# Gated attention and mixture block: batch 1's keys first, a third base summed early, copies and loads moved to other queues

## The chip, the cores and the metric

The kernel runs on one core of a Trainium2 chip. The metric is the device time of one execution in microseconds, the median over several runs. Five engines work side by side, each through its own instructions in order: TensorE (PE in the profile; PEld is its weight load), VectorE (DVE), ScalarE (ACT), GpSimd (POOL) and SyncE (SP). DMAs are issued by instructions that stand in the queue of SP, ScalarE or GpSimd.

## The reference

Eight batches of 256 tokens, 512 wide, all float32. Each goes through a gated attention and a gated mixture of experts:

```python
x = x + tanh(g_xattn) * attention(layernorm(x), context)
x = x + tanh(g_ffn) * mixture(layernorm(x))
```

The attention has 32 query heads and 8 key and value heads of 16. Queries come from the context and x together; keys and values once from x and once from the context. A query sees the 64 latest positions of both, with a bias that falls with distance, through one softmax. The mixture has 8 bases (gate, up and SiLU, 256 wide) that are mixed for each token by weights from a router (128 experts, the best 4), then a common down projection, and a shared expert of 512 that is handled as two more pieces of 256.

## The kernel before, in words

**Order of the work.** The program is written as generators: `attention(b)`, `project(b)`, `tail(b, t)`, `feed_forward(b)`, `first_weights()` and a few more. Each yields planned durations; `start` scales them to a stretch of planned time, and `run` always advances the generator that is due first. This planned time only decides the order in which instructions are written to the engines' queues. On the chip each engine takes its queue in order and waits at an instruction until its inputs and buffers are ready.

**Stages.** For a batch: `project` normalises x, transposes it, and forms keys (`pk`), queries (`pq`, four groups) and values (`pv`). Each result lies in a PSUM bank (`ps_one`, tag "one") until ScalarE has copied it out. `put_values` writes the values to `vpad`, and `diagonals` copies them by DMA (16 copies of 128 KB per batch) into `vbd`, a block-diagonal layout. `attention` takes 8 groups of scores (`sc`) in 16 steps: VectorE adds the bias and takes the maximum (L641), ScalarE does the exponential (L660), VectorE the reciprocal (L669), GpSimd the division (L672), VectorE the transpose (L685), TensorE the product with `vbd` (L707). `tail` projects the output (`po`, L866), normalises again, transposes (`tr_f`), and computes the router (`pl`, `pst`, `pc`). Then `feed_forward` computes 10 pieces (8 bases, 2 shared) with seven block products instead of eight, by sums of tokens (`sT`) and sums of weights.

**The first batches.** `project_first` does part of batch 0 directly. What is left of batch 0's projections, and then all of batch 1's, is a generator `rest` that `first_batch` (batch 0's attention) advances with `piece`, one part between two softmax steps at a time. Batch 0's attention thus runs beside the projections of batches 0 and 1, and the first feed-forward beside batch 1's attention and batch 2's projections.

**Sums of weights.** A piece of gate and up weights is four blocks of 256 KB (groups 1 to 4), and four sums of them are needed. `sub` forms a sum, `keep` stores it to DRAM; later batches load what is stored (`load_gu`). In `first_weights` bases 2, 0 and 1 are loaded and summed on GpSimd during the first softmax (`first_sums`). The pieces from 3 on are summed in the first feed-forward: `more` and `late` in `feed_forward` place `sub(k + 1, ...)`, two on VectorE and two on GpSimd, and the stores. Weight buffers are double; `after` loads piece i + 2 into a buffer as soon as TensorE has read piece i.

**The queues.** SP issues nearly all loads and stores from about 25 us on, in order: weights, stores of sums, the 16 copies to `vbd` of batches 1 to 7 and half of batch 0's (the other half is GpSimd's), and inputs of batches 2 to 7. ScalarE's queue issues the first weights and batch 1's inputs at the start. The line numbers in the profile before are those of this listing.

Of the kernel before, what the change touches and what calls it, by code (L numbers as in the profile page):

```python
# [37 lines left out]
def gated_block(  # L38
# [229 lines left out]

    def first_weights():

        for k in (2, 0, 1):
            for g in range(1, 5):
                load_gu(k, g)
            if k == 2:
                yield 2.0
                later["wd"] = weight(w_down, I, HID, "wd", nc.sync)


                later["sd"] = sd = const.tile([P, NSI // 2, HID], F32, tag="sd", name="sd")
                nc.sync.dma_start(  # L280
                    sd, sw_down.rearrange("(j o p) n -> o p j n", o=2, p=P)[1]
                )
            if k == 0:
                yield 5.5
                yield from first_sums(2)
        yield 1.0
        yield from first_sums(0)
        yield 1.0
        yield from first_sums(1)

    def first_sums(k):
        sub(k, 1, nc.gpsimd)
        yield 1.0
        sub(k, 3, nc.gpsimd)
        keep(k, 1)
        yield 1.0
        sub(k, 2)
        keep(k, 3)
        yield 1.0
        sub(k, 4)  # L300
        keep(k, 2)
        yield 1.0
        keep(k, 4)
        summed.add(k)
# [69 lines left out]
    def project_first():  # L374
# [62 lines left out]
        def rest():  # L437
            banks = [0]

            def own(name):  # L440
                banks[0] += 1
                if banks[0] % 2:
                    return other_bank(2, name)
                return ps_one.tile([P, 2 * T], F32, tag="one", name=name)

            pv = own("pv_0").rearrange("p (t s n) -> p t s n", t=NT, s=2)
            for t in range(NT):
                yield BEFORE if t == 0 else MORE
# [24 lines left out]
            ready.add("queries")  # L473
            yield from project(1, xns)
# [13 lines left out]
            yield fill[1]  # L488
            fill[1] = next(fill[0], None)

    def diagonals(qd, eng):


        for g in range(G):
            at = D * (1 - g % 2)
            eng.dma_start(
                vbd[g * Q : (g + 1) * Q, qd].rearrange("p a k r -> p a (k r)"),
                vpad[qd * Q : (qd + 1) * Q, :, at : at + 2 * HK * D],
            )
# [7 lines left out]
    def project(b, xns=None):  # L507
        def own():
            yield from hold(0.0 if b == 1 else GAP)
# [5 lines left out]
        if b > 1:  # L515
            while b > 2 and b - 3 not in stored:
                yield 0.5
            loaded[b] = load(b), load_context(b)
            yield 16.0
        xt, ctT = loaded[b]  # L520
        if xns is None:
# [2 lines left out]
            xns = normed()  # L524
            yield 3.0
        xnT = two.tile([P, NC, T], F32, tag="xo", name=f"xnT_{b}")
        if b == 1:
            yield BEFORE
        for t in range(NT):
            yield from own()  # L530
            evict = transposed(xnT, xns[t], t, f"x{b}", bank)
            yield AFTER if b == 1 else AFTER - 0.8
            evict()
            free()
            yield BEFORE if b == 1 else BEFORE + 0.8


        kT = two.tile([P, 2, 2, T], F32, tag="kT", name=f"kT_{b}")
        yield from own()
        pk = bank([P, 2, T], f"pk_{b}")  # L540
        for s, (w_sb, src) in enumerate(((wsk_sb, ctT), (wk_sb, xnT))):
            for c in range(NC):
                nc.tensor.matmul(  # L543
                    pk[:, s, :], lhsT=w_sb[:, c, :], rhs=src[:, c, :],
                    start=(c == 0), stop=(c == NC - 1),
                )
            yield AFTER if s else MORE
        for par in range(2):
            for s in range(2):
                nc.scalar.activation(  # L550
# [1 line left out]
                )  # L552
        free()
        yield BEFORE


        qT = two.tile([P, NB, G, Q], F32, tag="qT", name=f"qT_{b}")
# [34 lines left out]
    def attention(b):  # L592
# [185 lines left out]
        for u in range(2 * n + 4):  # L778
            i, j = divmod(u, 2)
            m = i // 2 - 1 if i >= 3 and i % 2 else None  # L780
            if j == 0:
                if i < n:
                    scs = score(i)
                elif m is not None:
                    scs = [bank(f"sc_{b}_{i}_{p}") for p in range(2)]
            if m is not None:
                values(m, j, pts[m], scs)
            exponentials()
            if i < n:
                nmax = memory(u)  # L790
            yield 1.0

            for step, ps in enumerate(((2,), (3,), (0, 1))):
                if u in (1, 2) and step < 2:
                    diagonals(2 * (u - 1) + step, nc.sync)
                exponentials()
                for p in ps:
                    if i < n:
                        soften(i, j, p, scs, prs[u], nmax, dens[u])
                if step == 0 and 0 <= u - 1 < 2 * n:  # L800
                    divide((u - 1) // 2, (u - 1) % 2, prs[u - 1], dens.pop(u - 1))
# [170 lines left out]
    def feed_forward(b):  # L972
# [120 lines left out]


        for k in range(PIECES):
            late = b == 0 and k > 2
            more = b == 0 and 2 < k + 1 < PIECES
            if k == NK:
                shT = one.tile([P, NSI, T], F32, tag="shT", name=f"shT_{b}")
            one_and_five(k)  # L1100
# [137 lines left out]
    project_first()  # L1238
    start(attention(0), 0.38, at=-0.585, total=70.0)
    start(after_diagonals(), 0.2, at=-0.535, total=1.0)  # L1240
    start(first_weights(), 0.39, at=-0.537, total=20.5)
    start(attention(1), 0.86, at=FIRST, total=74.1)
    at = -0.2
    while 0 not in sides:
# [52 lines left out]
```

## Time and profile before

| | |
|---|---|
| median of 3 runs | 1021.93 us (1018.09 to 1021.96) |
| profiled execution, its own time | 1023.29 us |
| its span | 1021.4 us |
| mean granted TensorE clock | 0.992 |
| busy: TensorE, VectorE, ScalarE, GpSimd | 989.7, 601.0, 442.0, 470.2 us |
| DMA, mean over the span | 188 GB/s |

The profile is one execution. A group's row gives line, engine, operation, output and input names, then busy time or start and length, and in brackets the wait just before it with the engine that ended it. SPq, ACTq and POOLq are the issues of DMAs; the rows of a queue's waits give the waiting line, what it waited for, the total, how often, and the longest. The time from issue to landing of a DMA is in the list of DMA issues. A clock below 1.00 in a window means that TensorE ran slower there.

### The profile page before, as it was taken

How to read it: one execution, taken by the hardware profiler on the slowest of the kernel's cores; microseconds unless marked ns; L12 is line 12 of the kernel's file. 1: busy time of each engine (PE TensorE's matmuls, PEld its weight loads, DVE VectorE, ACT ScalarE, POOL GpSimd, SP SyncE). 2: the span in 40 equal slices, each digit the busy share in tenths (PEclk: the TensorE clock that was granted, in tenths of full speed). 3: DMA queues.
4: the chain of work that ended last, by engine and by line, in shares of the span. 5: the costliest groups of instructions: out<-in, count | busy, mean ns of one | idle time of the engine just before them, and what ended most of it. 6: DMA issues, size and time to landing. Idle time of an engine off the chain costs nothing.

```text
span 1021.4 us, 27843 instructions
## 1 busy us (share of the span) xinstructions
PE 989.7 (97%) x10470; PEld 799.9 (78%) x10470; DVE 601.0 (59%) x2241; ACT 442.0 (43%) x1657; POOL 470.2 (46%) x892
## 2 busy tenths in 40 slices
PE   8888799899999999999999999999999999999998
PEld 8666687777888687886778868788787977787886
DVE  2764766757564675636855378544665466765453
ACT  3652454335542455415543255433554335442231
POOL 4773576734553255523644236342455225661341
PEclk9999999999999999999999999999999999999999
DMA  6942845569545694447844577455964468665891
GB/s 206 231 145 79 252 146 151 170 199 288 175 137 154 180 301 142 152 141 217 282 141 146 163 214 256 125 166 165 267 204 140 133 191 257 203 195 174 271 302 66
DMA packets 117302, 192.15 MB, mean 188 GB/s; under 512 B 12848, under 2 KB 34864, under 8 KB 117168
## 3 DMA queue, kind: packets, MB, share of 16 engines
q1 hardware_dynamic: 112672, 184.87, 58.9%
q10 hardware_dynamic: 4112, 4.46, 1.3%
q8 instruction: 83, 1.36, 0.5%
q0 software_dynamic: 384, 1.05, 0.5%
q14 instruction: 51, 0.42, 0.1%
HBM read 158.87 MB, written 14.68 MB: 170 GB/s over the span
## 4 chain that ended last, share of the span: by engine, by line
PE 87%; DVE 5%; issue 2%; POOL 2%; ACT 2%; DMA 1%; SPq 0%; ACTq 0%; DVEq 0%; POOLq 0%
PE m L1001 38%; PE m L1010 10%; PE pq L562 8%; PE sc L707 6%; PE po L866 5%; PE sc L628 5%; PE pd L1144 4%; PE pk L543 2%; PE pv L582 2%; PE pd L1147 2%; POOL pr L672 1%; PE pq L402 1%; PE pl L896 1%; DVE pr L641 1%; ACT pr L660 1%
## 5 line engine op out<-in xcount | busy, mean ns | idle before, releaser
L672 POOL TENSOR_SCALAR pr<-pr,rd 128x192 f32<-128x192 f32 (+2 forms) x512 | 210.9, 430 | 251.6 <-DVE rd L669 234.3
L660 ACT ACTIVATE pr<-pr,nm 128x192 f32<-128x192 f32 (+2 forms) x512 | 218.9, 430 | 110.0 <-DVE nm L641 58.7
L1001 PE MATMUL m<-w,sT 128*128 128x256 f32 x1024 | 253.1, 381 | 1.1 <-DMA w<-in_L_ffn_w_up 0.7
L1001 PEld LDWEIGHTS m<-w,sT 128*128 128x128 f32 x1024 | 194.5, 191 | 29.0 <-issue 1.2
L641 DVE CUSTOM_DVE_ANT_1 pr<-sc,nbias 128x192 f32<-128x192 f32 (+2 forms) x512 | 154.0, 322 | 99.8 <-PE sc L628 92.9
L1001 PE MATMUL m<-w,hT 128*128 128x256 f32 x768 | 204.9, 390 | 1.0 <-DVE u L1046 1.0
L1001 PEld LDWEIGHTS m<-w,hT 128*128 128x128 f32 x768 | 140.1, 191 | 25.6 <-issue 6.3
L1091 POOL TENSOR_TENSOR mixed<-mixed,th 128x256 f32<-128x256 f32 x112 | 81.2, 725 | 137.8 <-DVE th L1086 137.8
L685 DVE STREAM_TRANSPOSE pt<-pr 128x768 f32<-128x768 f32 (+2 forms) x128 | 111.5, 871 | 4.6 <-POOL pr L672 3.0
L660 ACT ACTIVATION_READ_ACCUMULATOR pr<-pr,nm 128x1 f32 x512 | 97.9, 191 | 0.0
L1047 POOL TENSOR_TENSOR m<-m,u 128x256 f32<-128x256 f32 x80 | 61.2, 765 | 67.8 <-DVE u L1046 58.9
L963 ACT ACTIVATE th<-m 128x256 f32<-128x256 f32 x80 | 30.8, 384 | 138.2 <-DVE up L1057 138.1
L707 PEld LDWEIGHTS sc<-pt,vbd 64*32 64x32 f32 x5120 | 61.1, 106 | 26.3 <-issue 14.2
L707 PE MATMUL sc<-pt,vbd 64*32 64x64 f32 (+2 forms) x5120 | 69.0, 229 | 9.1 <-DVE nm L641 5.2
L1069 DVE TENSOR_TENSOR gate<-u,m 128x256 f32<-128x256 f32 x80 | 33.3, 416 | 72.4 <-PE m L1001 66.9
L1057 DVE TENSOR_TENSOR up<-u,m 128x256 f32<-128x256 f32 x80 | 33.3, 417 | 67.6 <-PE m L1001 40.7
L628 PE MATMUL sc<-kT,qT 32*128 32x192 f32 (+2 forms) x1024 | 64.9, 336 | 4.6 <-DVE nm L641 4.1
L628 PEld LDWEIGHTS sc<-kT,qT 32*128 32x128 f32 x1024 | 45.1, 184 | 28.3 <-DVE nm L641 9.4
L963 ACT ACTIVATE th<-gate 128x256 f32<-128x256 f32 x80 | 33.2, 416 | 76.7 <-DVE gate L1069 76.7
L1010 PE MATMUL m<-sT,w 128*128 128x128 f32 x512 | 66.1, 278 | 0.0
L1010 PEld LDWEIGHTS m<-sT,w 128*128 128x128 f32 x512 | 62.3, 194 | 0.4
L1144 PE MATMUL pd<-sd,shT 128*128 128x512 f32 x128 | 61.5, 603 | 0.2 <-DVE shT L1080 0.2
(131 smaller groups left out, 1375.7 us busy)
## 6 DMA issues: line engine op xcount, KB each, us to landing
w<-s SPq DMA_DIRECT2D x284, 256.0 KB, 3.5
w<-in_L_ffn_w_gate SPq DMA_DIRECT2D x130, 256.0 KB, 3.1
w<-in_L_ffn_w_up SPq DMA_DIRECT2D x73, 256.0 KB, 4.0
vbd<-vpad SPq DMA_DIRECT2D x120, 128.0 KB, 3.2
s<-w SPq DMA_DIRECT2D x40, 256.0 KB, 3.4
w<-in_L_ffn_shared_w_gate SPq DMA_DIRECT2D x32, 256.0 KB, 2.7
w<-in_L_ffn_shared_w_up SPq DMA_DIRECT2D x18, 256.0 KB, 3.7
sd<-in_L_ffn_shared_w_down SPq DMA_DIRECT2D x16, 256.0 KB, 3.4
```

Source lines behind the costliest of these rows:

```text
L562: nc.tensor.matmul(pq, lhsT=wq_sb[:, c, g * P : (g + 1) * P], rhs=(ctT if c < NC else xnT)[:, c % NC, :], start=(c == 0), stop=(c == 2 * N ...
L628: nc.tensor.matmul(seen(scs[p][:, j * COLS : (j + 1) * COLS], qb), lhsT=qT[rows, qb].rearrange("p g q -> p (g q)"), rhs=kT[rows, par, :, f ...
L641: nc.vector.tensor_tensor_reduce(out=part, in0=seen(scs[p][:, j * COLS : (j + 1) * COLS], qb0 + j), in1=bass.AP(tensor=bias.tensor, offset ...
L660: nc.scalar.activation(part, part, AF.Exp, bias=nmax, scale=-1.0, accum_out=den)
L672: nc.gpsimd.tensor_scalar(part, part, rden[:, p : p + 1], 1.0, op0=ALU.mult, op1=ALU.mult)
L685: nc.vector.transpose(pt[:, u % 4].rearrange("p c (s k) -> p (c s) k", s=2)[:, :, lo:], pr.rearrange("p c (s k) -> p (c s) k", s=2)[:, :, ...
L707: nc.tensor.matmul(scs[gp][32 * c : 32 * (c + 1), 2 * COLS + lo * Q : 2 * COLS + hi * Q], lhsT=vbd[rows, kb % (P // Q), kb // (P // Q) * 2 ...
L963: nc.scalar.activation(th, gate, AF.Tanh, scale=0.5)
L1001: nc.tensor.matmul(dst, lhsT=sides_of[m][c], rhs=w[:, c, :], start=(first and c == 0), stop=(c == NC // 2 - 1), skip_group_check=True,)
L1010: nc.tensor.matmul(dst[:, cols], lhsT=w[:, c, cols], rhs=sides_of[m][c], start=(first and ic == c == 0), stop=(c == NC // 2 - 1), skip_gro ...
L1091: nc.gpsimd.tensor_add(mixed[t], mixed[t], th)
L1144: nc.tensor.matmul(po, lhsT=shT[:, ic, t * P : (t + 1) * P], rhs=down[ic], **flags)
```

## The change

Three parts, all in the stretch up to the end of the first feed-forward.

- **Base 3 early.** `first_weights` loads bases 2, 3, 0 and 1 and sums base 3 after base 2, on GpSimd. The first feed-forward then doesn't sum and store base 3, but loads its stored sums as it does for base 2. The planned stretch of `first_weights` is 0.40 and 25.5 units long instead of 0.39 and 20.5.
- **Keys first.** In `project(1)` the keys of the context are computed before x's transposes; these go to another PSUM bank (`other_bank(2)`) while the keys keep theirs, and the keys of x follow. The two banks that `rest` uses in turn change places, and one more pause stands ahead of batch 1's queries. For the other batches only a planned duration between the two halves of the keys changes.
- **Other queues.** The 16 `vbd` copies of batch 1 are issued half by ScalarE and half by GpSimd instead of SP. Batch 2's x and context are loaded by ScalarE's queue.

```diff
     def first_weights():
-        for k in (2, 0, 1):
+        for k in (2, 3, 0, 1):
             for g in range(1, 5):
                 load_gu(k, g)
...
-            if k == 0:
+            if k == 3:
                 yield 5.5
                 yield from first_sums(2)
+                yield 1.0
+                yield from first_sums(3)
...
             def own(name):
                 banks[0] += 1
-                if banks[0] % 2:
+                if banks[0] % 2 == 0:
                     return other_bank(2, name)
...
-    def diagonals(qd, eng):
+    def diagonals(qd, *engs):
         for g in range(G):
             at = D * (1 - g % 2)
-            eng.dma_start(
+            engs[g * len(engs) // G].dma_start(
...
-            loaded[b] = load(b), load_context(b)
+            eng = nc.scalar if b == 2 else nc.sync
+            loaded[b] = load(b, eng), load_context(b, eng)
...
+        if b == 1:
+            yield BEFORE
+            yield from own()
+            pk = bank([P, 2, T], f"pk_{b}")
+            keys(pk, 0)
+            for t in range(NT):
+                yield MORE
+                evict = transposed(
+                    xnT, xns[t], t, f"x{b}",
+                    lambda shape, name: other_bank(2, name).rearrange("p (c n) -> p c n", n=P),
+                )
+                yield AFTER
+                evict()
+            yield BEFORE
+            keys(pk, 1)
+            yield AFTER
+        else:
...
         free()
         yield BEFORE
+        if b == 1:
+            yield BEFORE
...
                 if u in (1, 2) and step < 2:
-                    diagonals(2 * (u - 1) + step, nc.sync)
+                    diagonals(2 * (u - 1) + step, *((nc.scalar, nc.gpsimd) if b == 1 else (nc.sync,)))
...
         for k in range(PIECES):
-            late = b == 0 and k > 2
-            more = b == 0 and 2 < k + 1 < PIECES
+            late = b == 0 and k > 3
+            more = b == 0 and 3 < k + 1 < PIECES
...
-    start(first_weights(), 0.39, at=-0.537, total=20.5)
+    start(first_weights(), 0.40, at=-0.537, total=25.5)
```

More of the change, by code (lines that the diff above doesn't have):

```diff
@@ L526, in project, with keys @@
         xnT = two.tile([P, NC, T], F32, tag="xo", name=f"xnT_{b}")
[L527 to L535, printed above, removed]
         kT = two.tile([P, 2, 2, T], F32, tag="kT", name=f"kT_{b}")
-        yield from own()
-        pk = bank([P, 2, T], f"pk_{b}")
-        for s, (w_sb, src) in enumerate(((wsk_sb, ctT), (wk_sb, xnT))):
+        def keys(pk, s):
+            w_sb, src = ((wsk_sb, ctT), (wk_sb, xnT))[s]
             for c in range(NC):
@@ L546, in project @@
                 )
-            yield AFTER if s else MORE
+        if b == 1:
[15 more added lines that the diff above has]
+        else:
+            for t in range(NT):
+                yield from own()
+                evict = transposed(xnT, xns[t], t, f"x{b}", bank)
+                yield AFTER - 0.8
+                evict()
+                free()
+                yield BEFORE + 0.8
+            yield from own()
+            pk = bank([P, 2, T], f"pk_{b}")
+            for s in range(2):
+                keys(pk, s)
+                yield AFTER
         for par in range(2):
```

## The prediction

> **What bounds the kernel now.** I read the totals first, then TensorE in time, then whatever ended its waits.
>
> ```profile
> span 1021.4 us, 27843 instructions
> PE 989.7 (97%) x10470; PEld 799.9 (78%) x10470; DVE 601.0 (59%) x2241; ACT 442.0 (43%) x1657; POOL 470.2 (46%) x892
> ```
>
> TensorE is busy for 97%, and nothing in the change removes a matmul. So only its waits can be won: 1021.4 - 989.7 = 31.7 us, and the slow-clock stretches after them. Busy time in windows (columns: length, TensorE, its weight loads, VectorE, ScalarE, GpSimd, granted clock, DMA share, GB/s) says where:
>
> ```profile
> 95.00:100.00 5.00, 4.48 (x17) 3.89 (x18) 4.06 (x22) 2.43 (x11) 1.48 (x6) 0.66 0.58 144
> 120.00:125.00 5.00, 1.11 (x4) 0.65 (x4) 3.58 (x11) 0.48 (x2) 1.10 (x2) 0.85 0.85 315
> 125.00:130.00 5.00, 3.65 (x69) 3.13 (x70) 4.92 (x17) 2.27 (x10) 4.84 (x5) 0.50 0.02 6
> 130.00:140.00 10.00, 10.00 (x62) 8.43 (x62) 6.69 (x23) 4.95 (x17) 6.92 (x12) 0.98 0.68 210
> 204.00:209.00 5.00, 5.00 (x63) 4.96 (x47) 1.02 (x2) 0.97 (x4) 0.85 (x2) 0.66 0.34 112
> ```
>
> Almost everything recoverable lies before 131 us; later windows show TensorE full, except around 200. In order of time (start, length, engine, line; bracket: wait before it and who ended it):
>
> ```profile
> 47.24 1.99 PE L543 MATMUL pk<-ctT,wsk 128*128 128x256 f32 x8 [1.58 <-ACT xnT L205]
> 94.19 0.65 PE L204 MATMUL tr_f<-ident,xn_f 128*128 128x128 f32 x4 [1.29 <-DVE xn_f L190]
> 119.98 1.13 PE L1001 MATMUL m<-w,sT 128*128 128x256 f32 x4 [0.73 <-DMA w<-in_L_ffn_w_up]
> 126.35 1.55 PE L707 MATMUL sc<-pt,vbd 64*32 64x96 f32 x64 [5.24 <-DVE nm L641]
> 203.81 0.63 PE L707 MATMUL sc<-pt,vbd 64*32 64x96 f32 x37 [3.64 <-issue]
> ```
>
> The 5.24 us is explained by VectorE and SP:
>
> ```profile
> 121.31 0.69 DVE L953 TENSOR_TENSOR w<-w,w 128x512 f32<-128x512 f32 x1 [3.50 <-DMA w<-in_L_ffn_w_up]
> 114.78 0.38 SPq L349 DMA_DIRECT2D w<-in_L_ffn_w_up  x1
> ```
>
> A sum of base 3 sits in VectorE's queue and waits for a w_up piece issued at 114.78 and landed at 121.29 (6.5 us; 4.0 is the median). Behind it stand batch 2's statistics, softmax steps and the transposes TensorE needs.
>
> **Part 1: base 3 summed early.** The two VectorE sums (0.69 us) and two GpSimd sums (1.27) leave the first feed-forward. Four GpSimd sums come into the first softmax: 4 x 1.27 = 5.1 us. In the feed-forward base 3 now has seven loads instead of four and no stores. The wait at 119.98, that of 5.24 and the slow clock after them go. From 118.1 to 130.9 (12.8 us) TensorE did four half-blocks at 0.86 us and one values group at 0.94, 4.4 us in all. **Gain 8.4 us.** The later sums (base 4 on) come a block after, when the DMA has caught up. This is the firmest term.
>
> **Part 2: the stretch up to the first feed-forward** (before: starts at 96.8). Keys of the context come before the transposes, so TensorE no longer waits 1.58 us for their copy; the two transposes now follow each other in one bank and the second waits some 1.4 us for the first's copy. That is a wash. What sets the end is the chain of softmax divisions on GpSimd:
>
> ```profile
> 43.98 1.62 POOL L672 TENSOR_SCALAR pr<-pr,rd 128x192 f32<-128x192 f32 x4 [4.39 <-DVE rd L669]
> 46.22 1.62 POOL L672 TENSOR_SCALAR pr<-pr,rd 128x192 f32<-128x192 f32 x4 [0.61 <-DVE rd L669]
> 77.03 1.62 POOL L672 TENSOR_SCALAR pr<-pr,rd 128x192 f32<-128x192 f32 x4
> ```
>
> In the changed order eleven sums instead of eight stand ahead of the last division: 3 x 1.27 = 3.8 us. But GpSimd waited 12.0 us for reciprocals between 40 and 82, and step 12's scores move ahead of one query projection (2.0 us). Walking both queues with these durations (base 0's loads, now behind base 3's stores, land near 71), I get the last division at 76.7 against 77.03, and its transposed block at 79.3 against 79.7. So the cover is just enough; without it the stretch would be 3.8 us longer. From 79.3 the matmul work left is 1.7 (values), 1.9 + 3.5 + 1.9 (query half, output projection, query half), 0.2, 1.9, 0.7, 0.1, 0.4, 1.8, 0.9 and 0.4 of queue turn-round: start of the feed-forward at about 94.2. The waits of 1.29 and 0.68 us disappear because a query half and the value projection now stand behind the output projection. **2.6 us**, plus 1.3 for the clock (0.74 granted over 97 to 102 us: 0.26 x 5). **Gain 3.9 us**, bounds 0 and 7.
>
> **Part 3: copies and loads on other queues.** SP loses 16 issues of vbd (0.60 us) and two loads (0.38 and 0.46): 10.4 us. POOL gets 8 vbd (0.55 each, 4.4 us), at a time when it waits; ScalarE gets 8 (bounded by 0.55 and 0.60) and the loads: 5.6 us. Two things count on ScalarE. First, it computes nothing while it issues. Second, in the program as built each DMA also waits for the landing of an unrelated, earlier one that shares its completion semaphore. Before shows what this does, at the start:
>
> ```profile
> 7.56 1.85 ACTq L112 DMA_DIRECT2D x<-in_x  x1
> SPq L496 <- DMA x<-in_x: 4.6, 1, 4.6
> ```
>
> The issue of x held ScalarE for 1.85 us instead of 0.38 to 0.60, and a vbd copy, which doesn't read x, waited 4.6 us for it. SP could bear that. On ScalarE the exponentials, the copies of u and m5 and the tanh stand behind. Counting from the feed-forward's start (t), with landings of 3.1 (weights), 3.2 (vbd) and 5.0 (x at 111.6): the first two vbd t+1.9 to 3.1; u and m5 copies to 3.7; third 4.3; fourth waits for a weight issued once the first block has run and goes to 5.1; two exponentials, m7, the token selection's copy, two exponentials to 7.4; x and context to 8.4; fifth waits for the fourth's landing, 9.0; sixth 9.8; tanh 10.2; seventh waits for x, t+12.4, to 13.0; eighth 13.6; then four exponentials (1.8) and the copies of the second base's u and m5 to t+16.0. TensorE, unhindered, wants those copies at t+10.5. **Loss 5.5 us.** Bounds: 2, if issues fit ScalarE's own gaps; 18, if the four chained landings (fourth vbd, its successor, x, the last weight) each take the longest seen (8.0 for vbd, 8.9 for x).
>
> Here two rules of the Trainium skill bear. "DMA: Bandwidth & Descriptors" (section Issuing engines are not separate DMA queues) says that all queues share the same 16 engines, and another issuer saves only issue time. The row agrees with that against the change: from 115 to 120 the DMA share is 0.97 at 338 GB/s. By the rule part 3 earns nothing by itself, since VectorE's wait was already removed by part 1; I give it no gain. Had SP's 10.4 us been worth their full length, the sum would be far larger. "TensorE: Matmul & The Clock Gate" (Part 1: The HAM clock gate) says an idle window of about 3.4 us halves the clock until a window of equal length has been busy. The row: after the wait of 3.64 the clock was 0.66 over 5 us (1.7 lost), but after 1.29 + 0.68 also 0.66. By the rule the new wait, split into about 1.4 and 3.5 by a block that runs between, may cost nothing; by the row it costs 1.7. I take the row. **Loss with clock 7.2 us.**
>
> The rest has one answer: the swapped bank parity and the extra pause only place the same matmuls.
>
> Sum: -8.4 - 3.9 + 7.2 = -5.1 us. The profiled execution took 1023.29 us, 1.9 more than its span; it becomes 1018.2. The median of the runs shown is 1021.93, so the forecast is **1016.8 us**. The 3.64 us at 203.81 ("issue": nothing the profile shows) belongs to no part; if it is absent (1018.09 among the three times suggests that it can be), 5 us more go, if absent in both nothing.
>
> **The rivals.**
>
> *ScalarE's issues are hidden.* For it: ScalarE was idle 5 of 15 us in 95 to 110, and DMA is lighter after part 1's stores are gone. Against: the waits on landings are not issue time. With a loss of 2: -8.4 - 3.9 + 2 = -10.3, some 1011.5; with the code stall also gone 1006.5.
>
> *The first softmax pays for the sums.* If base 0's loads land late or the divisions fall 3.8 us back, part 2 gives nothing or loses: -8.4 + 7.2 + 0 to 3.8 is -1 to +3, about 1021. For it: GpSimd at 8.34 of 10 between 70 and 80. Against: its 12.0 us of waiting. That includes the case in which removing the wait at 121 only exposes another at the same place.
>
> *Slower: ScalarE held by landings.* The mechanism is the issue of the seventh vbd, held until x has landed, ahead of the exponentials. It decides from a loss of 12.3 us on (8.4 + 3.9), that is, if the copies of u and m5 come at t+23 instead of 16. With 18 + 1.7 the sum is +7.4: 1029. For it: 16 small-packet copies, x, context and seven more loads run together, and landings have reached 8.9. Against: medians of 3 to 5 even where the DMA was at 0.9 of its time.
>
> **How the numbers follow.** A measurement of this kernel can tell about 0.5%, 5.1 us. Forecast case 0.45 (own range 1012 to 1021; it stands at the bound itself, so 0.25 faster and 0.20 within), hidden issues 0.30 (all faster), first softmax pays 0.12 (0.02 faster by an absent code stall, 0.08 within, 0.02 slower), held by landings 0.13 (0.02 within, 0.11 slower). Faster 0.25 + 0.30 + 0.02 = 0.57; within 0.20 + 0.08 + 0.02 = 0.30; slower 0.02 + 0.11 = 0.13. The range leaves out about 0.2: low 1006 (hidden issues and no code stall), high 1025 (half of the landings case).
>
> **What would show it.** Right: no VectorE sum that waits for w_up near 120, and no TensorE wait of 5 us there; the feed-forward's first matmul near 94 at clock 1.0; ScalarE's DMA issues of 1 to 3 us each for the seventh vbd and around it, and TensorE waiting 3 to 5 us in all for "m" or "sc" some 10 to 18 us later, released by ScalarE. Wrong: the first feed-forward starting after 97; ScalarE issues of 0.6 each (second case); TensorE waiting over 10 us between 95 and 125 (fourth case); or the base 3 pieces themselves arriving late.

## The result, and the profile after

The changed kernel takes 1023.55 us (median of 20 runs, 1020.15 to 1030.38), the kernel before 1021.24 (20 runs, 1018.09 to 1023.0). The ratio is 1.0031, with a 95% interval of 1.0018 to 1.0044: slower by 0.3%, where 1016.8 us was forecast. The profiled execution took 1024.72 us; its span is 1022.9.

The totals of the changed kernel (busy time, share of the span, instructions) show that TensorE's work is the same and that 32.7 us of the span are again outside it (31.7 before):

```profile
span 1022.9 us, 27842 instructions
PE 990.2 (97%) x10470; PEld 800.6 (78%) x10470; DVE 599.1 (59%) x2239; ACT 441.2 (43%) x1657; POOL 474.1 (46%) x902
```

The windows of the changed kernel (columns as in the prediction: length, TensorE, weight loads, VectorE, ScalarE, GpSimd, clock, DMA share, GB/s). The hole of 120 to 130 is gone; there is one at 110 to 120 instead, with the DMA's share at 1.05 and 1.09, and a smaller one after 130:

```profile
95.00:100.00 5.00, 5.00 (x53) 4.68 (x53) 2.85 (x15) 1.96 (x7) 3.08 (x4) 1.00 0.28 105
110.00:115.00 5.00, 1.62 (x5) 1.37 (x6) 1.65 (x8) 0.38 (x1) 1.77 (x4) 0.90 1.05 327
115.00:120.00 5.00, 3.99 (x10) 2.69 (x9) 3.00 (x12) 4.85 (x20) 1.79 (x4) 0.50 1.09 282
120.00:125.00 5.00, 5.00 (x35) 3.95 (x34) 3.15 (x18) 2.14 (x12) 3.51 (x7) 0.92 0.92 239
130.00:140.00 10.00, 8.39 (x104) 6.75 (x107) 8.65 (x29) 6.51 (x25) 6.95 (x14) 1.00 0.27 80
204.00:209.00 5.00, 2.89 (x158) 2.39 (x148) 4.26 (x13) 0.94 (x3) 1.31 (x4) 0.72 0.73 262
```

TensorE in order of time (start, length, line; bracket: the wait before it and who ended it):

```profile
47.24 0.66 PE L204 MATMUL tr_x<-ident,xn_a 128*128 128x128 f32 x4 [1.50 <-ACT xnT L205]
51.02 2.05 PE L732 MATMUL sc<-pt,vbd 64*32 64x96 f32 x112 [1.55 <-DVE pt L710]
52.99 3.45 PE L535 MATMUL pk<-xnT,wk 128*128 128x256 f32 x8
82.56 2.14 PE L732 MATMUL sc<-pt,vbd 64*32 64x96 f32 x144 [2.63 <-DVE rrd L937]
99.30 1.03 PE L1027 MATMUL m<-w,hT 128*128 128x256 f32 x4
113.38 3.15 PE L1027 MATMUL m<-w,sT 128*128 128x256 f32 x8 [3.95 <-DVE th L994]
117.54 2.07 PE L1027 MATMUL m<-w,hT 128*128 128x256 f32 x4 [1.01 <-ACT m L1060]
133.38 1.15 PE L732 MATMUL sc<-pt,vbd 64*32 64x96 f32 x64 [1.61 <-DVE nm L666]
```

The feed-forward starts at 99.30, not near 94 (96.81 before). The VectorE sum that waited for w_up is gone, and with it the wait of 5.24. Two waits at 113 and 117 have come. They are ScalarE's, as its own rows show (an ACTq row is the issue of a DMA, an ACT row a computation):

```profile
111.02 1.27 ACTq L498 DMA_DIRECT2D vbd<-vpad  x2
112.40 0.38 ACT L989 ACTIVATE th<-m 128x256 f32<-128x256 f32 x1 [5.32 <-issue]
112.87 2.18 ACTq L498 DMA_DIRECT2D vbd<-vpad  x2
115.10 0.46 ACT L685 ACTIVATE pr<-pr,nm 128x192 f32<-128x192 f32 x1 [2.32 <-DMA w<-in_L_ffn_w_gate]
117.12 0.37 ACT L1060 COPY m<-m 128x256 f32<-128x256 f32 x1
```

ScalarE stood idle for 5.3 us before the tanh at 112.40, behind the load of the context and two copies that could not be issued yet. The exponential at 115.10 waited, behind two more copies, until a load of weights had landed that neither it nor the copies read. The copy of m5 came 17.8 us after the feed-forward's start (forecast 16.0). The median times from issue to landing between 97 and 122 us were 3.2 (copies), 5.0 (x) and 6.3 us (context) in the kernel before. Now they are:

```profile
vbd<-vpad ACTq DMA_DIRECT2D x8, 128.0 KB, 7.4
x<-in_x ACTq DMA_DIRECT2D x1, 512.0 KB, 7.1
ctT<-in_ctx ACTq DMA_DIRECT2D x1, 512.0 KB, 11.9
```

For all that follows I use two marks: **t**, the first `m` matmul of the first feed-forward, and **E**, block 4 of base 2 (a block is one of the seven products of a piece), which ends the disturbed stretch (before: 130.87; changed kernel: 134.46). The changed kernel loses 2.5 us up to t and 1.1 from t to E, where the forecast had -2.6 and -2.5 (parts 1 and 3, and the clock of part 2).

### The profile page after: what moved, and what is told of

Its sections match the earlier page's. It is cut to its first block, busy times and chain, and to the rows that moved or that the text cites. A ratio compares the mean times of both kernels' runs of the same rounds, so it can differ in the third digit from the quotient of the medians.

```text
span 1022.9 us, 27842 instructions
## 1 busy us (share of the span) xinstructions
PE 990.2 (97%) x10470; PEld 800.6 (78%) x10470; DVE 599.1 (59%) x2239; ACT 441.2 (43%) x1657; POOL 474.1 (46%) x902
## 4 chain that ended last, share of the span: by engine, by line
PE 85%; DVE 5%; DMA 2%; ACT 2%; POOL 2%; SPq 1%; issue 1%; ACTq 0%; POOLq 0%; DVEq 0%
PE m L1027 37%; PE m L1036 9%; PE pq L587 9%; PE sc L732 6%; PE po L892 5%; PE sc L653 5%; PE pd L1170 4%; PE pv L607 3%; PE pk L535 2%; PE pd L1173 2%; ACT pr L685 1%; PE pq L404 1%; POOL w L979 1%; DMA w<-in_L_ffn_w_gate 1%; POOL pr L697 1%
## 5 line engine op out<-in xcount | busy, mean ns | idle before, releaser
L697 POOL TENSOR_SCALAR pr<-pr,rd 128x192 f32<-128x192 f32 (+2 forms) x512 | 208.4, 427 | 228.0 <-DVE rd L694 204.0
L1095 DVE TENSOR_TENSOR gate<-u,m 128x256 f32<-128x256 f32 x80 | 33.2, 415 | 80.5 <-PE m L1027 71.1
L732 PE MATMUL sc<-pt,vbd 64*32 64x96 f32 (+2 forms) x5120 | 71.2, 235 | 8.3 <-DVE pt L710 3.7
```

Source lines behind the costliest of these rows:

```text
L697: nc.gpsimd.tensor_scalar(part, part, rden[:, p : p + 1], 1.0, op0=ALU.mult, op1=ALU.mult)
L732: nc.tensor.matmul(scs[gp][32 * c : 32 * (c + 1), 2 * COLS + lo * Q : 2 * COLS + hi * Q], lhsT=vbd[rows, kb % (P // Q), kb // (P // Q) * 2 ...
```

## The experiments

All times are medians; the kernel before, on the same chip beside them, took 1020.75 to 1021.77. In the table, "copies" is the queue of batch 1's sixteen `vbd` copies, "loads" that of batch 2's x and context; "base 0's loads first" means base 3 early with base 0's loads ahead of base 3's sums. The marks t and E come from one profiled execution, whose own time is in the last column; it can lie several us from the median (e9: 1010.8 against 1015.6). After E all eighteen profiles take between 887.7 and 892.2 us, so a profile's own time follows its E.

| kernel | base 3 early | keys first | copies | loads | t | t to E | time | profiled |
|---|---|---|---|---|---|---|---|---|
| before | no | no | SP | SP | 96.8 | 34.1 | 1021.2 | 1023.3 |
| changed | yes | yes | ScalarE, GpSimd | ScalarE | 99.3 | 35.2 | 1023.6 | 1024.7 |
| e1 | yes | yes | SP | SP | 94.9 | 35.7 | 1023.0 | 1021.0 |
| e2 | yes | no | SP | SP | 99.3 | 27.0 | 1017.4 | 1018.4 |
| e3 | no | no | ScalarE, GpSimd | ScalarE | 98.3 | 35.4 | 1025.3 | 1025.3 |
| e4 | no | yes | SP | SP | 92.0 | 35.5 | 1020.5 | 1018.4 |
| e5 | yes | yes | ScalarE, GpSimd | ScalarE | 98.6 | 34.4 | 1024.5 | 1023.6 |
| e6 | yes | yes | ScalarE, GpSimd | SP | 99.8 | 36.8 | 1027.4 | 1028.0 |
| e7 | yes | yes | GpSimd | SP | 96.3 | 33.2 | 1020.6 | 1019.7 |
| e8 | base 0's loads first | yes | GpSimd | SP | 94.5 | 33.2 | 1019.0 | 1021.8 |
| e9 | yes | yes | left out | SP | 94.6 | 26.1 | 1015.6 | 1010.8 |
| e10 | base 0's loads first | yes | GpSimd | SP, later | 94.1 | 35.2 | 1022.9 | 1021.7 |
| e11 | yes | yes | ScalarE, GpSimd | ScalarE, later | 96.8 | 35.0 | 1022.4 | 1022.4 |
| e12 | base 0's loads first | yes | GpSimd | SP, near 80 | 95.0 | 27.9 | 1013.4 | 1012.6 |
| e13 | base 0's loads first | yes | SP | SP, near 80 | 95.7 | 29.3 | 1015.8 | 1016.2 |
| e14 | base 0's loads first | no | SP | SP, near 80 | 97.1 | 27.2 | 1016.8 | 1017.6 |
| e15 | base 0's loads first | yes | ScalarE, GpSimd | SP, near 80 | 94.1 | 32.5 | 1020.5 | 1016.9 |
| e16 | base 0's loads first | yes | SP, GpSimd | SP, near 80 | 93.3 | 27.2 | 1012.7 | 1011.4 |

### e1: the queues back

```diff
-            eng = nc.scalar if b == 2 else nc.sync
+            eng = nc.sync
...
-                    diagonals(2 * (u - 1) + step, *((nc.scalar, nc.gpsimd) if b == 1 else (nc.sync,)))
+                    diagonals(2 * (u - 1) + step, nc.sync)
```

> The changed kernel with batch 1's copies and batch 2's loads back on SP; TensorE's order is the same. Theory A (ScalarE held by landings is what part 3 costs): TensorE's waits of 3.95 for th and 1.01 for m in the first feed-forward go, with the slow clock between 115 and 120; from the first m matmul to the third piece 15 us again as before instead of 22.4; about 1016 us, 7 under the changed kernel and 5 under the kernel before. Rival B (the 16 engines of the DMA are full and the landings are late from any queue): the wait moves to SP's weight loads, TensorE waits as long for w; 1021 to 1024.

Measured: 1022.96 us, ratio 1.0033 (1.0020 to 1.0046). My theory A falls: ScalarE's waits are gone, and the time is the same as the changed kernel's. TensorE's rows of e1, then SP's:

```profile
112.73 1.03 PE L1027 MATMUL m<-w,hT 128*128 128x256 f32 x4
122.87 2.07 PE L1027 MATMUL m<-w,sT 128*128 128x256 f32 x4 [9.11 <-DMA w<-in_L_ffn_w_up]
```

```profile
113.22 4.08 SPq L498 DMA_DIRECT2D vbd<-vpad  x4
117.36 0.58 SPq L351 DMA_DIRECT2D w<-in_L_ffn_w_up  x1
```

TensorE runs unhindered to 113.8 (it starts the third piece at 108.31 instead of 121.73; counted from t, 9.1 us sooner), and then stands for 9.11 us before block 3 of base 2, the third piece, whose w_up was issued only at 117.36, behind the sixteen copies. What ScalarE's queue lost before 122, SP's queue loses at 122.

### e2, e3, e4: each part alone

e2 has the change's lines of `first_weights`, `late`, `more` and its start; e3 those of `diagonals`, its call and batch 2's loads; e4 those of `project(1)`, the banks' parity and the added pause. Their cores, against the kernel before:

```diff
-        for k in (2, 0, 1):
+        for k in (2, 3, 0, 1):
...
-            late = b == 0 and k > 2
+            late = b == 0 and k > 3
```

```diff
-                    diagonals(2 * (u - 1) + step, nc.sync)
+                    diagonals(2 * (u - 1) + step, *((nc.scalar, nc.gpsimd) if b == 1 else (nc.sync,)))
```

```diff
+            keys(pk, 0)
+            for t in range(NT):
+                yield MORE
+                evict = transposed(
```

> The kernel before with base 3's sums early and nothing else. Theory A: the first feed-forward starts 2 to 4 us later than in the kernel before (eleven GpSimd sums ahead of the last division), and the waits of 0.73 and 5.24 near 120 go, worth 6.5 to 8.4; sum -3 to -6, 1016 to 1018. Rival C (the early sums are paid back in full in the first softmax): start 6 or more later, 1021 or more.

Measured: 1017.38 us, ratio 0.9970 (0.9961 to 0.9979), as theory A had it. The start is 2.5 us later and the stretch to E 7.1 us shorter; TensorE's waits near 122 in e2:

```profile
121.85 1.13 PE L1005 MATMUL m<-w,sT 128*128 128x256 f32 x4 [0.49 <-DMA w<-in_L_ffn_w_up]
123.39 1.15 PE L710 MATMUL sc<-pt,vbd 64*32 64x96 f32 x64 [0.40 <-DVE nm L644]
```

Part 1 does what was forecast. But look at the first row: block 3 of base 2 still starts when its w_up lands, at 121.85, as it did at 119.98 in the kernel before. There is no slack left behind the sum that was removed.

> The kernel before with only the queues changed. Theory A: start of the first feed-forward as before (97), then ScalarE's issues hold the second pair of u and m5 copies; TensorE loses 5 to 8 us by 112, of which some is hidden again since the VectorE sum's wait near 121 hangs on SP, whose w_up is issued earlier; 1021 to 1029, not below 1021. Rival B (SP's issue time is what binds): w_up issued some 5 us earlier, VectorE's wait of 3.50 and TensorE's of 5.24 go, 1015 to 1018.

Measured: 1025.25 us, ratio 1.0050 (1.0032 to 1.0068). Part 3 alone loses, in the middle of what was expected of A. The longest of its new waits behind ScalarE is at the token selection:

```profile
109.02 0.39 PE L940 MATMUL pc<-mix,selT 128*128 128x8 f32 x2 [3.53 <-ACT selT L935]
```

From t to the third piece TensorE takes 19.6 us instead of 14.8, and by E most of that is hidden again (35.4 against 34.1).

> The kernel before with batch 1's context keys ahead of its two transposes and nothing else. Theory A: a wash, start of the first feed-forward within 1 us of 96.8, 1020 to 1022. Rival D (the new order itself slows the clock at 53 us and so makes the first softmax late): start at 98 to 100, 1023 to 1025.

Measured: 1020.45 us, ratio 1.0005 (0.9992 to 1.0018): the time of theory A, but not its reason. The start was to stay within 1 us of 96.8; it is at 91.98, 4.8 us earlier. A new wait stands at one place:

```profile
91.98 1.03 PE L1025 MATMUL m<-w,hT 128*128 128x256 f32 x4
109.78 1.03 PE L1025 MATMUL m<-w,hT 128*128 128x256 f32 x4
117.49 2.08 PE L1025 MATMUL m<-w,sT 128*128 128x256 f32 x4 [6.68 <-DMA w<-in_L_ffn_w_up]
```

It is the same block 3 of base 2 again. In this profile, which is the fastest of 14 executions, E is still 3.4 us earlier than before; the median shows no gain, and where a typical execution loses the rest is not shown. Added up, e2 and e4 should give -3.9 us together; in e1 they give +2.1. So the parts do not add: e1 starts 4.4 us before e2, but block 3 of base 2 gets its w_up no earlier (122.87 against 121.85), and TensorE spends the gain waiting.

### e5: the changed kernel once more

> The changed kernel once more, for a second profile on the chip on which the parts are compared. If its late first feed-forward (99.3 in the first profile) belongs to the clock of that one execution, it starts near 95 as with the queues back (94.9), and the two waits behind th and m, 5 us, are there again. If it belongs to the kernel, it starts at 99 again. Time 1022 to 1025.

Measured: 1024.48 us; t at 98.57, and the two waits are there again (4.06 for th, 0.96 for m). The late start was not an accident of the first profile alone, though it varies: seven executions with the same instructions up to t (changed, e1, e5, e6, e7, e9, e11) start between 94.6 and 99.8, mean 97.2.

### e6: the loads back on SP, the copies where the change put them

```diff
-            eng = nc.scalar if b == 2 else nc.sync
+            eng = nc.sync
```

> The changed kernel with batch 2's two loads back on SP; the sixteen copies stay on ScalarE and GpSimd. Theory F (the wait for w_up and the wait for th are one and the same delay, put on SP or on ScalarE by where the copies are issued; on ScalarE the seventh copy waits for x): with the loads on SP the seventh copy waits for nothing late, the waits behind th and m shrink from 5.0 to 2 to 3 us; 1018 to 1021. Rival E (the 16 DMA engines are full from 105 to 120, and who issues makes no difference): 1022 to 1025, TensorE waits 5 us or more again.

Measured: 1027.38 us, ratio 1.0046 (1.0030 to 1.0063). A miss: TensorE waited 2.84 for th and 2.16 for m, no less than in the changed kernel (5.0), and 1.56 for the token selection. So x's landing on ScalarE's queue is not what holds the copies there.

### e7 and e8: the copies on GpSimd, then base 0's loads first

```diff
-                    diagonals(2 * (u - 1) + step, *((nc.scalar, nc.gpsimd) if b == 1 else (nc.sync,)))
+                    diagonals(2 * (u - 1) + step, nc.gpsimd if b == 1 else nc.sync)
```

That is e7 (with the loads on SP, as in e6). e8 has besides:

```diff
-            if k == 3:
-                yield 5.5
-                yield from first_sums(2)
-                yield 1.0
-                yield from first_sums(3)
+            if k in (3, 0):
+                yield 5.5 if k == 3 else 1.0
+                yield from first_sums(2 if k == 3 else 3)
```

> The changed kernel with all sixteen copies of batch 1 on GpSimd's queue and batch 2's loads on SP: no DMA is issued by ScalarE, and SP is rid of the copies. Theory F: neither the wait for w_up (9.11 with the copies on SP) nor those behind th and m (3.95 and 1.01) appear; w_up issued by 112 instead of 117.4; 1014 to 1017. Rival E: w_up issued early lands late, TensorE waits over 5 us for it or for vbd; 1021 to 1024. Rival G (GpSimd's 16 x 0.55 = 8.8 us of issues delay its sums of m and the divisions): TensorE waits 3 to 5 us for nm or m behind GpSimd; 1018 to 1021.

Measured: 1020.64 us, ratio 0.9990 (0.9975 to 1.0004). The time lies in rival G's range, but the wait is rival E's, and F falls. Here w_up was issued early, at 106.81 instead of 117.36, and TensorE waited all the same. The windows, SP's row, one TensorE row and two rows of the DMA's list (window 97 to 122) of e7:

```profile
110.00:115.00 5.00, 3.66 (x17) 2.92 (x16) 3.00 (x15) 2.07 (x11) 4.84 (x11) 1.00 1.07 240
115.00:120.00 5.00, 1.70 (x8) 1.14 (x6) 4.60 (x16) 2.58 (x11) 3.43 (x8) 0.89 1.06 260
```

```profile
106.81 0.44 SPq L351 DMA_DIRECT2D w<-in_L_ffn_w_up  x1
121.69 2.07 PE L1027 MATMUL m<-w,sT 128*128 128x256 f32 x4 [5.00 <-DMA w<-in_L_ffn_w_up]
```

```profile
q0 software_dynamic: 768, 2.10, 39.5%
...
w<-s SPq DMA_DIRECT2D x8, 256.0 KB, 9.6
```

SP's queue is not late any more; the transfers are. A stored sum needs 9.6 us to land (3.3 in the kernel before), and the copies alone (q0: packets, MB, share of 16 engines) take 39.5% of the 16 engines over 25 us: 9.9 us. Rival G is seen only in a small way (1.34 us for th). Still, e1 and e7 differ in the copies' queue alone and their intervals lie apart: with the copies on GpSimd instead of SP the ratio is 0.4% lower, some 4 us.

> As the one before, and base 0's four loads issued ahead of base 3's sums and stores instead of behind them. GpSimd's wait of 3.1 to 3.4 us for base 0's w_up (ahead of the last two divisions) goes. If that wait sets the start of the first feed-forward, it comes 2 to 3 us earlier than in the one before, and so does the end; if TensorE's order or the clock sets it, no difference.

Measured: 1019.03 us, ratio 0.9984 (0.9974 to 0.9994). GpSimd's row of base 0's first sum, in the changed kernel and in e8, shows what was removed:

```profile
74.54 1.27 POOL L979 TENSOR_TENSOR w<-w,w 128x512 f32<-128x512 f32 x1 [3.13 <-DMA w<-in_L_ffn_w_up]
79.86 1.64 POOL L697 TENSOR_SCALAR pr<-pr,rd 128x192 f32<-128x192 f32 x4
```

```profile
69.72 1.27 POOL L979 TENSOR_TENSOR w<-w,w 128x512 f32<-128x512 f32 x1
76.51 1.62 POOL L697 TENSOR_SCALAR pr<-pr,rd 128x192 f32<-128x192 f32 x4
```

The last division starts at 76.51 instead of 79.86. The six kernels with keys first and base 0's loads first start between 93.3 and 95.7, mean 94.5: 2.7 us before the mean of the seven above. From t to E nothing changes (33.2), so E comes earlier with the start. In time the intervals of e7 and e8 overlap.

### e9: the copies left out

This kernel leaves out batch 1's copies, so its output is not that of the reference; it shows only what they cost.

```diff
-                if u in (1, 2) and step < 2:
+                if u in (1, 2) and step < 2 and b != 1:
```

> As e7 (copies on GpSimd, loads on SP), with batch 1's sixteen copies left out (batch 1's attention then reads old values; 2.1 MB less to move between 97 and 122). Theory H (the stretch from 97 to 122 is bound by the 16 DMA engines, and whatever is gained ahead of it is spent waiting for its end): TensorE's waits of 1.34 for th and 5.00 for w_up go, from the first m matmul to the fourth block of the third piece 27 us as with base 3 alone, instead of 33.2; 1012 to 1015. Rival I (the wait comes from the order of the instructions or from the buffers of the weights, not from the amount moved): 33 us again, 1019 to 1021.

Measured: 1015.58 us, ratio 0.9951 (0.9932 to 0.9971). From t to E 26.1 us instead of 33.2, and no wait of TensorE for th or w_up between 82 and 119. Windows of e9:

```profile
110.00:115.00 5.00, 5.00 (x36) 4.08 (x35) 4.84 (x22) 3.62 (x16) 2.33 (x7) 1.00 0.86 282
115.00:120.00 5.00, 3.28 (x89) 2.43 (x89) 4.96 (x19) 1.53 (x7) 4.59 (x8) 1.00 0.42 150
```

The order of instructions and the buffers are those of e7. So rival I falls; what went is 2.1 MB, and the copies' issues on GpSimd. The time is a little above what theory H gave.

### e10 and e11: batch 2's loads later

```diff
+            if b == 2:
+                yield 10.0
...
-            yield 16.0
+            yield 6.0 if b == 2 else 16.0
```

(e10 on e8, e11 on the changed kernel.)

> As e8 (copies on GpSimd, base 0's loads first), with batch 2's x and context (1.05 MB) loaded after the third piece's weights instead of before them. Theory H: 1.05 of 6.3 MB, 4 of 25 us of the DMA, leaves the full stretch; w_up lands 4 us earlier, the wait of 4.94 falls to 0 to 2; 1013 to 1016. If the loads only collide with the next weights, TensorE waits later for w or for batch 2's transposes, 1018 to 1020. Rival I: 1019.

Measured: 1022.88 us, ratio 1.0017 (1.0007 to 1.0027), slower than e8, and a miss for H's 1013 to 1016. The wait for w_up fell as theory H has it, from 4.94 to 2.50, but a new one came. VectorE's row and TensorE's in e10:

```profile
121.52 0.69 DVE L179 BATCH_NORM_STATS2 st_a<-x 128x6 f32<-128x512 f32 x1 [5.93 <-DMA x<-in_x]
```

```profile
127.84 1.50 PE L734 MATMUL sc<-pt,vbd 64*32 64x96 f32 x64 [4.36 <-DVE nm L668]
```

Batch 2's statistics stand in VectorE's queue ahead of the softmax steps, and now wait for the late x. The lighter stretch can't be judged by this run.

> The changed kernel (copies on ScalarE and GpSimd) with batch 2's loads, still on ScalarE, the same 10 steps later. Theory H: ScalarE's copies and the copies' landings come sooner, TensorE's waits behind th and m fall from 5.0 to 2 or 3, and no wait for w_up takes their place; 1018 to 1021. If ScalarE's issues cost the time whatever the load of the DMA: 1022 to 1025.

Measured: 1022.37 us, ratio 1.0015 (1.0000 to 1.0029). TensorE waits 1.29, 0.54 and 4.34 us behind ScalarE and the tanh, 6.2 in all. A miss for H.

### e12 to e16: batch 2's loads ahead of the full stretch

Between 80 and 97 us the DMA has little to do (share 0.24 in e8), and batch 2's buffers are free. So x and context go there, between the stores of bases 0 and 1:

```diff
         yield from first_sums(0)
+        loaded[2] = load(2), load_context(2)
...
+            if b != 2:
-            loaded[b] = load(b, eng), load_context(b, eng)
+                loaded[b] = load(b, eng), load_context(b, eng)
```

> As e8 (copies on GpSimd, base 0's loads first), with batch 2's x and context loaded near 80 us, between base 0's and base 1's stores, where the DMA's share was 0.3, and not in the full stretch from 97 to 122. Theory H (amount moved in that stretch): the end of the stretch comes 3 to 4 us earlier and, unlike with the later loads, VectorE's statistics wait for nothing; from the first m matmul to the fourth block of the third piece 29 to 30 us instead of 33.2; 1014 to 1016. Rival K (what counts is the copies' own issue and landings, not the sum of the bytes): 33 us again, 1019.

Measured: 1013.38 us, ratio 0.9930 (0.9907 to 0.9952). Faster than both kernels. Two windows of e12, then SP's issue of w_up and the block that waited 9.11 in e1, first in e8 and then in e12:

```profile
80.00:85.00 5.00, 5.00 (x153) 3.79 (x136) 2.58 (x9) 0.43 (x2) 1.16 (x1) 1.00 0.73 231
110.00:115.00 5.00, 4.09 (x18) 2.94 (x16) 4.11 (x15) 2.96 (x14) 4.92 (x11) 1.00 1.05 251
```

```profile
105.86 0.49 SPq L351 DMA_DIRECT2D w<-in_L_ffn_w_up  x1
119.91 2.07 PE L1027 MATMUL m<-w,sT 128*128 128x256 f32 x4 [4.94 <-DMA w<-in_L_ffn_w_up]
```

```profile
104.03 0.52 SPq L352 DMA_DIRECT2D w<-in_L_ffn_w_up  x1
116.06 1.13 PE L1029 MATMUL m<-w,sT 128*128 128x256 f32 x4 [1.27 <-DMA w<-in_L_ffn_w_up]
```

The stretch is still full, but the block gets its w_up 3.9 us earlier than in e8. Of these, 1.8 us are SP's: x and context no longer stand ahead of w_up in its queue. The other 2.0 are a shorter transfer, 12.0 us from issue to the block's start instead of 14.1. Half of the bytes that e9 left out (1.05 MB against 2.1) give 5.3 us from t to E where e9 gained 7.1, with every copy on GpSimd as in e8. So rival K falls.

> As the one before, with the copies on SP's queue as in the kernel before. If the amount moved is all that counts, the same time as the one before within 2 us (1014 to 1017). If SP's issues still hold w_up, the wait for it is 3 to 5 us longer than there, 1018 to 1020.

Measured: 1015.78 us, ratio 0.9938 (0.9915 to 0.9961). The wait for w_up is 3.58 us instead of 1.27 and the stretch to E 1.4 us longer; the intervals of e12 and e13 overlap. What SP's issues cost here, 2.4 us by the medians, is not told apart from nothing.

> The kernel before with base 3's sums early, base 0's loads first and batch 2's loads near 80; TensorE's order of keys and transposes, and the copies on SP, as before. With base 3 alone no wait for w_up was left (0.5 us), so theory H gives nothing for the lighter stretch but 1 to 2 us for the earlier divisions: 1015 to 1017, and not better than the two before.

Measured: 1016.78 us, ratio 0.9957 (0.9944 to 0.9971). As expected: without keys first TensorE comes late enough for the landing, so the lighter stretch gives nothing from t to E (27.2 against 27.0 in e2); the start is 2.2 us earlier than in e2.

> As e12 and e13 (base 0's loads first, batch 2's loads near 80), with the copies on ScalarE and GpSimd as in the changed kernel: the three differ in the copies' queue alone. If ScalarE's queue costs by itself, because copies that wait for landings stand ahead of its activations, TensorE waits 3 us or more for activations after 100 and the time is 3 to 7 us over e12: 1016 to 1020. If only the amount moved counts: 1012 to 1015.

Measured: 1020.52 us, ratio 0.9993 (0.9981 to 1.0005). e12 and e15 differ in the copies' queue alone, and their intervals lie apart: 0.6% or 6 to 7 us. TensorE's waits in e15, in a profile that is the fastest of 22 executions:

```profile
101.55 0.39 PE L966 MATMUL pc<-mix,selT 128*128 128x8 f32 x2 [1.15 <-ACT selT L961]
105.98 1.97 PE L1029 MATMUL m<-w,sT 128*128 128x256 f32 x8 [1.35 <-POOL pr L699]
111.22 1.13 PE L1029 MATMUL m<-w,hT 128*128 128x256 f32 x4 [3.28 <-ACT m L1062]
```

So ScalarE's queue does cost by itself, once no later wait covers it: the stretch to E is 4.6 us longer than in e12, though TensorE no longer waits for w_up.

> As e12, with the copies half on SP and half on GpSimd. Between the two by the queue's part (e12 1013.4, e13 1015.8): 1013 to 1016; if fewer issues on each queue help both (the wait of 0.71 for th behind GpSimd, that of 3.58 for w_up behind SP): 1011 to 1013.

Measured: 1012.73 us, ratio 0.9926 (0.9897 to 0.9955), four runs. Not distinguishable from e12; it has the smaller wait at th (none) and 2.27 for w_up. e12 and e16 are the fastest of all, 0.7% under the kernel before; e13, e14, e2 and, by little, e8 are also faster than both kernels.

## Why the prediction was wrong

The two traces show where the forecast and the changed kernel part (us; the forecast's own terms, put on the kernel before: 20.7 is 14.8 less the 1.3 of part 2's clock plus the 7.2 of part 3; 10.9 is 19.3 less the 8.4 of part 1):

| stretch | before | forecast | changed |
|---|---|---|---|
| up to t | 96.8 | 94.2 | 99.3 |
| t to the start of the third piece | 14.8 | 20.7 | 22.4 |
| from there to E | 19.3 | 10.9 | 12.7 |
| E to the end | 890.5 | 890.5 | 888.4 |

Most of the miss is the start, part 2's term: 5.1 us. The stretches of parts 3 and 1 miss by 1.7 and 1.8 us in the same direction, and 2.1 us come back after E. The experiments show a second mistake, which this table hides: the terms don't keep their worth when another one is taken away.

**Part 2 (forecast -3.9, start at 94.2): the step that failed.** The walk of the two queues had base 0's loads land near 71 and the last division at 76.7. In the profile base 0's first sum begins at 74.54, after a wait of 3.13 us for w_up, and the last division at 79.86. SP takes up these loads only after the eight stores of bases 2 and 3, and base 3's follow GpSimd's sums:

```profile
50.69 17.54 SPq L983 DMA_DIRECT2D s<-w  x8
68.28 0.93 SPq L351 DMA_DIRECT2D w<-in_L_ffn_w_gate  x2
```

The rival in which the first softmax pays had this cause, and a start after 97 stood among the signs of being wrong. With the loads first (e8, e10, e12, e13, e15, e16) the start is at 94.5 in the mean, as forecast. What the walk left out is a slow clock: the new order has waits of 1.50 and 1.55 us about 4 us apart, and the keys of x after them took 3.45 us (granted clock 0.50 from 50 to 55) where I had 1.99. In the seven executions with the same instructions up to t, the keys of x end between 53.3 and 56.6 us, base 0's first sum begins between 71.3 and 75.3 and the feed-forward starts between 94.6 and 99.8, in nearly the same order. The two with the earliest keys, e1 and e9, start at 94.9 and 94.6, as forecast. That the clock makes the rest late is read from this order; it was not tried by itself. The mean of the seven is 97.2; if they are alike, some 2 us of the 5.1 are the luck of the profiled execution.

"That is a wash" was wrong too, in the other direction: alone, the new order starts 4.8 us earlier (e4, one profile of each kernel). What an earlier start is worth depends on the copies' queue. With half of them on ScalarE (changed kernel, e5, e11) or all on GpSimd (e7, e8) the stretch from t to E keeps its length, 34.4 to 35.2 and 33.2 us, and E comes about as much earlier as the start. With the copies on SP, TensorE meets a landing that moves less than the start (e4: 2.5 of 4.8 us) or not at all (e1 against e2), and that much of the gain is spent waiting.

**Part 1 (forecast -8.4): right in size, wrong in what it assumed behind it.** From the third piece to E it gives 6.5 us in the changed kernel; alone it shortens the stretch from t to E by 7.1 us (e2). But the sentence that the waits at 119.98 and of 5.24 "go" with the sum holds only as long as TensorE comes late. I looked for what else is late at VectorE and SP's w_up of base 3, and not at the row just before: the 0.73 us at 119.98 said that TensorE was already waiting for another load, base 2's w_up. That landing was the next limit, without any slack. The rival of the first softmax included the case that removing the wait "only exposes another at the same place"; e1, with 9.11 us, is that case. The seven loads in place of four were named in the forecast but not priced: 3 x 256 KB are 0.79 MB, at the 253 GB/s that the kernel before moved between 97 and 122 some 3.1 us (an estimate) of a stretch that from 100 to 120 was full at shares of 0.85 to 0.97. That this is what moved w_up from 117.49 (e4) to 122.87 (e1) was not tried by itself.

**Part 3 (forecast +7.2): the mechanism right, its place in the sum wrong.** TensorE's new waits came to 5.7 us (forecast 5.5), and the slow clock cost 3.0 us instead of 1.7 (the blocks at 113.38, 117.54 and 119.41 took 3.15, 2.07 and 1.74 us, where 1.89, 1.03 and 1.03 is full speed). But taking the loss away gains nothing, because then TensorE waits 9.11 us at base 2's w_up (e1: the same time). The loss is paid, with 6 to 7 us, when that wait has been removed (e15 against e12). The story of the seventh copy that waits for x was too special: with x on another queue the waits were as long (e6). "It computes nothing while it issues" is not what the rows of the changed kernel show either: during the issue at 100.10, of 0.72 us, two exponentials began at 100.24 and 100.57. And the zero for SP's relief was too small: e7 against e1 is worth some 4 us.

**The sum.** Its three terms were added as if each kept its worth without the others. They lie side by side, against a stretch in which the 16 DMA engines are nearly full: 6.3 MB between 97 and 122 in the kernel before and in the changed one, at a share of 0.86 and 0.93, and above 1.0 from 100 to 120 in e7 and e8. The rule I quoted from the Trainium skill ("DMA: Bandwidth & Descriptors", Issuing engines are not separate DMA queues) spoke of just that, and I used it only to deny SP's 10.4 us a gain. e7 bears it out in the main: w_up was issued 10.6 us earlier than in e1, and counted from t the block that needs it came only 2.5 us earlier. It isn't the whole, as e12, e13 and e15 show: the amount is the same in all three, and the time is 1013.4, 1015.8 and 1020.5.

**The 3.64 us at 203.81,** given to no part, are not in the profile of the changed kernel, but a loss of that kind is: from 204 to 209 TensorE is busy for 2.89 of 5.00 us, at a clock of 0.72. The two profiles differ little over this place.

What stays open: how much of the gains of e9 and e12 comes from the bytes and how much from a freed queue, GpSimd's in e9 and SP's in e12. Also open is what the start of the changed kernel would be at full clock. That base 3 alone is 3.5 us faster in time while E comes 4.6 us earlier is no contradiction: the two profiled executions differ by 4.9 us (1023.3 and 1018.4).

## What to carry to other kernels

Before gains of several parts are added, ask which landing each of them runs into: work whose wait is ended by a DMA can keep its time however early the work before it is done (e1), and a small wait for a load (0.7 us here) marks the next limit. In a stretch where the DMA's share is near 1, another queue for the issues mostly moves the wait (9.1 us behind SP's issues, 5.0 behind GpSimd's). Moving a megabyte out of it, to an earlier place with a share of 0.3, gave 5 us; moved later, its consumer's queue was held. Issues that must wait for landings stand worst on an engine whose short operations others wait for, as ScalarE here.

## What the runs showed of the hardware

- Landings stretch when more is asked of the DMA at once: stored sums of 256 KB took 3.3 us (median) in the kernel before and 9.6 in e7, context 6.3 and 15.7, at nearly the same 6.3 MB in 25 us. In e7 the loads were issued earlier, and the DMA's share was 1.02 instead of 0.86.
- Two short waits near one another often went with the slow clock. Keys of x, eight matmuls: 1.99 us after waits of 1.49 and 0.39 (e4), 2.5 to 3.5 us in all thirteen profiled kernels with keys first and base 3 early, where the second wait was 0.76 to 1.66. The waits don't decide it alone: in the old order, after waits of 0.7 and 1.58 us, the keys of the context took 1.99 us in the kernel before and 3.11 to 3.36 in e2, e3 and e14. The idle window of about 3.4 us ("TensorE: Matmul & The Clock Gate", The HAM clock gate) is longer than any wait there; none reaches 2 us.
- The same instructions up to t took from 94.6 to 99.8 us in seven executions, nearly in the order in which the keys of x ended. The granted clock between 35 and 40 us, 0.55 in the changed kernel and 0.82 in e5, differs from one to the next as well. One profile of a start is known to about 3 us only, more than a part of this change is worth.
